# VectorE's order written out by hand while a two-layer kernel scans, and row scatters that no longer wait for each other

## The chip, the cores and the metric

The kernel runs on one core of one Trainium2 chip. The metric is the time of one execution on the device in microseconds (us). Three runs of the kernel before gave a median of 2133.94 us (2133.84 to 2136.27). The engines are named as the profile names them: PE (TensorE matmuls), PEld (TensorE weight loads), DVE (VectorE), ACT (ScalarE), POOL (GpSimd) and SP (SyncE, which here only issues DMAs).

## The reference

Two transformer-like layers run over 4 batches of 1024 tokens with 128 features. Each layer is an attention-like part and a mixture of experts, each behind a layer norm that is shifted, scaled and gated per batch. Layer 0 is causal attention with 16 heads, then 8 experts of which each token takes 2, without a capacity. Layer 1 is a selective scan (a Mamba block), then 8 experts, top 2, each with room for 512 tokens per choice. The part that the change is about is the scan:

```python
deltaA   = exp(delta[..., None, None] * A)                  # (B, S, 128, 16)
deltaB_u = delta[..., None, None] * B_sel[:, :, None, :] * u[..., None]
h   = a_t * h + bu_t                                        # for each token t in order
y_t = einsum('bdn,bn->bd', h, c_t)
...
x = x + ga * _L1_attn_ref(h, ...)    # silu(conv(x W_in)) scanned, gated by silu(z), times W_out
x = x + gb * _L1_ffn_ref(h, ...)     # router, top 2, gather, gelu experts, weighted sum
```

## The kernel before, in words

The residual `x` stays in SBUF as 32 tiles of 128 tokens. There are three stretches.

**Attention** (to about 1428 us of the profiled execution). Eight stages, one per batch and half of the heads. Layer 0's experts of a batch run beside the attention of the next one: `sort_tokens` (L331) ranks the tokens of a batch by expert and scatters their rows, 16 indirect DMAs issued by POOL (L385), into a DRAM tensor `f_in[b]` that was filled with zeros at the start (L491); `Blocks` (L393) multiplies 23 blocks of 128 rows; `return_steps` (L271) gathers the results back and DVE adds them to `x` (L278). The sort of batch 3, its blocks and the returns of batches 2 and 3 are left to the scan stretch. POOL also scales the probabilities (L586) that PE transposes (L595). All 16 scatters write one tensor, so each waits until the one before has landed.

**Scans** (1474 to 1906 us). A batch has 32 chunks: 16 groups of 8 features by 16 states, each for two halves of 512 tokens. A chunk (`scan`, L897) is a PE matmul that spreads `du` over the states into a PSUM bank `pu`, a DVE multiply by `bb` in place (L906), an ACT exponential `da` (L908), the DVE scan `h` (L910), for the first half an ACT copy of its last column into `carry` (L912), and a POOL multiply `hc` by `cc` (L914). There are four banks for `pu` and three buffers each for `da` and `h`. Four `hc` are summed by PE into `py` (`collected`, L917). After 16 chunks `scan_output` (L924) gates `py` into `yh` (L927), multiplies by `W_out` (`pw`), gates again (L932), and POOL adds to `x` (L934).

Other work goes beside the chunks, as generators that a `Beside` (L1159) advances by so many steps per pair of chunks from pair `at` on: `scan_inputs` of the next batch (L839: norm, convolution, softplus, `du`), `dispatch` of the batch before (L936: norm, router, top 2, positions, 16 scatters), the sort of batch 3, `first_blocks` (L774) and the returns. After the last pair of a batch every generator is run to its end (`f.rest()`) before the next batch's first chunk is written down.

**Layer 1's experts** (from 1941 us). `dispatch_last` handles the last four tiles, then 16 expert runs and the last blocks follow.

The order of instructions on every engine is made by the framework's scheduler from what the program writes down and its own estimate of durations; each engine then runs its list strictly in that order. The hand only breaks in with `next_to` and `issue_after`.

Of the kernel before, what the change touches and what calls it, by code (L numbers as in the profile page):

```python
# [49 lines left out]
def adaln_two_layers(ctx: ExitStack, tc: tile.TileContext, I: dict, out: bass.AP):  # L50
# [90 lines left out]
    def norm_steps(t0, nt, dst, on_act=True):  # L141
# [13 lines left out]
        yield  # L155

# [114 lines left out]
    def return_steps(src, t0, nt, placei, w, pool, bufs, store=False):  # L271

        came = []

        def add():
            for t, k, y in came:
                xt = x[:, t0 + t, :]
                nc.vector.scalar_tensor_tensor(xt, y, w[:, k, t : t + 1], xt, ALU.mult, ALU.add)  # L278
            if store and came and came[0][0] % 2 == 1:
                at = t0 + came[0][0] - 1  # L280
                nc.sync.dma_start(outv[:, at : at + 2, :], x[:, at : at + 2, :])

        for t in range(nt):
            here = []
            for k in range(2):
                y = pool.tile([P, D], F32, tag="fy", bufs=bufs, name="fy")
                nc.gpsimd.indirect_dma_start(
                    out=y,
                    out_offset=None,
                    in_=src[:, :],  # L290
                    in_offset=bass.IndirectOffsetOnAxis(ap=placei[:, k, t : t + 1], axis=0),
                )
                here.append((t, k, y))
            add()
            came = here
            yield
        add()

    kept = {}
# [11 lines left out]
    def first_returns(b, pool, bufs):  # L311
        _, placei, w = kept[b]
        return return_steps(f_out[b], b * TB, TB, placei, w, pool, bufs)
# [17 lines left out]
    def sort_tokens(b, kept, pool, ps, tag, xtag="fxn"):  # L331
# [5 lines left out]
        yield from feature_steps(xn, hT, ps, modT[0][:, 4, b : b + 1], modT[0][:, 3, b : b + 1])  # L337
        pl = ps.tile([P, TB, NE], F32, tag="m", name="fpl")
# [8 lines left out]
        pin = ps.tile([P, TB + 1, NE], F32, tag="m", name="fpin")  # L347
# [34 lines left out]
        kept[b] = expert, placei, w  # L382
        for t in range(TB):
            for k in range(2):
                nc.gpsimd.indirect_dma_start(  # L385
                    out=f_in[b][:, :],
                    out_offset=bass.IndirectOffsetOnAxis(ap=placei[:, k, t : t + 1], axis=0),
                    in_=xn[:, t, :],
                    in_offset=None,
                )  # L390
                yield

    class Blocks:  # L393


        def __init__(self, b, pool, ps, banks, rest):
            self.b, self.expert, self.pool, self.ps, self.rest = b, kept[b][0], pool, ps, rest
            self.banks = itertools.cycle(banks)
# [4 lines left out]
        def load(self, n):  # L403
# [3 lines left out]
            nc.sync.dma_start(self.xe[:, :m], rows_in[:, 3 * n : 3 * n + m])  # L407

        def turn(self, n):

            m = min(3, NB - 3 * n)
            tp = self.ps[0].tile([P, 3, P], F32, tag=self.ps[1], name="ftp")
# [8 lines left out]
        def first(self, j):  # L421

            if j >= NB:
                return
            w, r = self.ws[len(self.held)], j % 3
            bank, tag = next(self.banks)
# [5 lines left out]
            nc.scalar.activation(sg, pf[:, 0:2], AF.Tanh, scale=0.5)  # L432
            nc.vector.scalar_tensor_tensor(sg, sg, 1.0, pf[:, 0:2], ALU.add, ALU.mult)
# [4 lines left out]
            self.held.append((pf, am, ar))  # L438

        def second(self, j):  # L440

            if j >= NB:
                return
            w, r = self.ws.pop(0), j % 3
            pf, am, ar = self.held.pop(0)
            if r == 0:
                self.ye = self.pool.tile([P, 3, D], F32, tag="fye", bufs=1, name="fye")
            mm(nc, pf[:, 3], ar, w[:, 4 * P : 5 * P], stop=False)
            mm(nc, pf[:, 3], am, w[:, 3 * P : 4 * P], start=False)
            nc.vector.tensor_mul(self.ye[:, r], pf[:, 3], gate_b0[:, self.b, :])  # L450
# [12 lines left out]
    with ExitStack() as es:  # L463
# [23 lines left out]
        for slots in f_in + xd + [g_in]:  # L487
            flat = slots.rearrange("(p r) d -> p (r d)", p=P)
            for at in range(0, flat.shape[1], 512):
                n = min(512, flat.shape[1] - at)  # L490
                nc.sync.dma_start(flat[:, at : at + n], mask[:, :n])  # L491
# [169 lines left out]
        for at, (b, c) in enumerate(stages):  # L661
# [47 lines left out]
            if c == 0 and b > 0:  # L709
                blocks = Blocks(b - 1, ab, (ps_m, "m"), [(ps_m, "m")], rest)  # L710
# [26 lines left out]
    with ExitStack() as es:  # L737
# [36 lines left out]
        def first_blocks(b):  # L774

            blocks = Blocks(b, fb, (ps_g, "g"), [(ps_g, "g"), (ps_m, "d")], rest)
            for j in range(NB):
                if j % 3 == 0:
                    blocks.turn(j // 3)
                blocks.first(j)  # L780
                if j > 0:
                    blocks.second(j - 1)
                yield
            blocks.second(NB - 1)
# [54 lines left out]
        def scan_inputs(b):  # L839
# [23 lines left out]
            for t in range(TB):  # L863
                mm(nc, pd[:, t : t + 1], xc[:, t * P : (t + 1) * P], m_dt)
            r = mb.tile([P, TB], F32, tag="sp_r", name="sp_r")
# [31 lines left out]
        def scan(pair, g, carry, dt, du, bb, cc):  # L897

            tok = slice(g * 512, (g + 1) * 512)
            hcs, pus = [], []  # L900
            for c in pair:
                pu = ps_u.tile([P, 512], F32, tag=f"pu{next(turn) % 4}", name="pu")
                mm(nc, pu, spread[:, c].rearrange("p a n -> p (a n)"), du[:, tok])
                pus.append(pu)
            for c, pu in zip(pair, pus):
# [7 lines left out]
                hcs.append(wide("hc", 10, 512))  # L913
                nc.gpsimd.tensor_mul(hcs[-1], h, cc[:, tok])  # L914
            return hcs
# [8 lines left out]
        def scan_output(b, g, py, sz):  # L924
# [3 lines left out]
            pw = ps_m.tile([P, 4, D], F32, tag="d", name="pw")  # L928
            for q in range(4):
                mm(nc, pw[:, q], y[:, q * P : (q + 1) * P], m_out)  # L930
            u = mb.tile([P, 4, D], F32, tag="wide_gated", bufs=1, name="wide_gated")
            nc.vector.tensor_mul(u, pw, gate_a1[:, b : b + 1, :].to_broadcast([P, 4, D]))  # L932
            xt = x[:, b * TB + 4 * g : b * TB + 4 * g + 4, :]
            nc.gpsimd.tensor_add(xt, xt, u)  # L934

        def dispatch(b, t0, nt):  # L936
# [30 lines left out]
            mm(nc, pall.rearrange("p t k e -> p (t k e)"), ones, mine.rearrange("p t k e -> p (t k e)"))  # L967
            yield
# [42 lines left out]
        def dispatch_last():  # L1011
# [63 lines left out]
            for t in range(nt):  # L1075
                for k in range(2):
                    nc.gpsimd.indirect_dma_start(
                        out=g_in[:, :],
                        out_offset=bass.IndirectOffsetOnAxis(ap=placei[:, k, t : t + 1], axis=0),
                        in_=hx[:, t, :],  # L1080
                        in_offset=None,
                    )
# [7 lines left out]
        sent = []  # L1090

        def last_experts():
# [11 lines left out]
            def rows(q):  # L1104
                n = min(4, nb - q)
                ins[q] = eb.tile([P, 4, D], F32, tag="gxe", name="gxe")
                nc.sync.dma_start(ins[q][:, :n], rows_in[:, q : q + n])
# [51 lines left out]
        class Beside:  # L1159


            def __init__(self, steps, at, n):
                self.steps, self.at, self.n, self.value, self.ended = steps, at, n, None, False
# [15 lines left out]
        inputs = Beside(scan_inputs(0), 0, 1)  # L1179


        sending = None
        output = None
        for b in range(B):
            sz, xc, *scanned = inputs.rest()
            carry = mb.tile([P, NCH], F32, tag="carry", name="carry")
            beside, among = [], []
            if b == 0:
                beside.append(Beside(first_returns(B - 2, db, 6), 4, 1))
                beside.append(Beside(sort_tokens(B - 1, kept, db, ps_m, "hT2", "hx"), 2, 4))  # L1190
                beside.append(Beside(shift_and_scale(), NCH - 3, 1))
            if b == 1:
                among.append(Beside(first_blocks(B - 1), 1, 1))
            if b == 2:
                beside.append(Beside(first_returns(B - 1, db, 6), 0, 2))
            if sending is not None:
                beside.append(sending)
            if b + 1 < B:
                inputs = Beside(scan_inputs(b + 1), 5 if b == 2 else 2, 3 if b == 2 else 2)
                beside.append(inputs)  # L1200
            hcs, late = [], None
            for m in range(NCH):

                g, n = divmod(m, NCH // 2)
                hcs += scan([4 * (2 * n % 4 + r) + n // 2 for r in range(2)], g, carry, *scanned)
                for f in among:
                    if m >= f.at:
                        f.take(1)
                if n == 1:

                    if late is not None:
                        late()
                        late = None
                        if b + 1 == B:
                            beside.append(Beside(dispatch(b, 0, TB - NL), m + 1, 8))
                    elif output is not None:
                        output()
                        output = None
                if n == 2:
                    py = ps_y.tile([P, 512], F32, tag="py", name="py")  # L1220
                    mm(nc, py, skip, xc[:, g * 512 : (g + 1) * 512], stop=False)
                if n % 2 == 1 and n > 1:
                    collected(n // 2 - 1, hcs[:4], py)
                    hcs = hcs[4:]
                if n == NCH // 2 - 1:

                    def late(b=b, g=g, hcs=hcs, py=py, sz=sz):
                        collected(3, hcs, py)
                        scan_output(b, g, py, sz)

                    hcs = []
                for f in beside:
                    if m >= f.at:
                        f.take(f.n)
                for f in among:
                    if m >= f.at:
                        f.take(1)
            output = late
            for f in beside + among:
                f.rest()  # L1240
            if b + 1 < B:
                sending = Beside(dispatch(b, 0, TB), 2, 3)
            if b == 1:
                fw_scope.close()
                gw = ctx.enter_context(tc.tile_pool(name="gw", bufs=1, side="right"))
# [186 lines left out]
```

## Time and profile before

| | us |
|---|---|
| median of 3 runs | 2133.94 |
| profiled execution, own time | 2139.09 |
| its span, first to last instruction | 2137.4 |
| PE, DVE, POOL, ACT busy in the span | 1792.8, 1323.7, 994.6, 947.3 |
| scan stretch, first chunk to last `h` | 1474 to 1905.6 = 431.6 |
| last `h` to the first expert matmul `ph` | 1905.6 to 1941.1 = 35.5 |
| DVE multiply `pu` (L906), scan `h` (L910) | 0.684, 1.207 or 1.269 each |
| POOL `hc` (L914), one indirect DMA issue (L385) | 1.275, 0.99 each |

Busy times are unions of an engine's instructions; the rest of a stretch is idle time, and the profile names what ended each idle time. PEclk is the granted TensorE clock as a share of full speed.

### The profile page before, as it was taken

How to read it: one execution, taken by the hardware profiler on the slowest of the kernel's cores; microseconds unless marked ns; L12 is line 12 of the kernel's file. 1: busy time of each engine (PE TensorE's matmuls, PEld its weight loads, DVE VectorE, ACT ScalarE, POOL GpSimd, SP SyncE). 2: the span in 40 equal slices, each digit the busy share in tenths (PEclk: the TensorE clock that was granted, in tenths of full speed). 3: DMA queues.
4: the chain of work that ended last, by engine and by line, in shares of the span. 5: the costliest groups of instructions: out<-in, count | busy, mean ns of one | idle time of the engine just before them, and what ended most of it. 6: DMA issues, size and time to landing. Idle time of an engine off the chain costs nothing. (4 is left out here: it accounts for less than half of the span.)

```text
span 2137.4 us, 29054 instructions
## 1 busy us (share of the span) xinstructions
PE 1792.8 (84%) x8957; PEld 971.7 (45%) x8957; DVE 1323.7 (62%) x4000; ACT 947.3 (44%) x2073; POOL 994.6 (47%) x1277
## 2 busy tenths in 40 slices
PE   5399999998999989899989899967769757857984
PEld 3144344444455445455535446533335423325774
DVE  5356556665667666566766566655858888882243
ACT  1145454554445374355455454544456345423321
POOL 1334534436523643633363652344654675772254
PEclk9699999999999999999989999987979877867997
DMA  6400101001222200222210122210003230002345
GB/s 221 137 1 15 36 1 28 23 1 54 72 75 68 70 4 27 73 59 68 78 36 1 51 75 65 61 44 10 26 30 98 71 113 13 8 21 88 99 144 149
DMA packets 103756, 123.59 MB, mean 58 GB/s; under 512 B 15024, under 2 KB 68656, under 8 KB 103600
## 3 DMA queue, kind: packets, MB, share of 16 engines
q1 hardware_dynamic: 84256, 99.01, 15.7%
q0 software_dynamic: 8192, 16.74, 2.4%
q10 hardware_dynamic: 11152, 5.97, 0.9%
q8 instruction: 71, 1.16, 0.2%
q14 instruction: 85, 0.70, 0.1%
HBM read 67.85 MB, written 32.90 MB: 47 GB/s over the span
## 5 line engine op out<-in xcount | busy, mean ns | idle before, releaser
L586 POOL TENSOR_SCALAR pr<-pr,den 128x32 f32<-128x32 f32 (+31 forms) x512 | 353.2, 705 | 301.9 <-DVE den L583 295.9
L580 ACT ACTIVATE pr<-pr,nb 128x32 f32<-128x32 f32 (+31 forms) x512 | 371.6, 727 | 194.5 <-DVE nb L567 191.5
L595 PE MATMUL pt<-ident,pr 128*128 128x128 f32 x2304 | 341.9, 283 | 46.4 <-POOL pr L586 37.0
L46 PE MATMUL sc<-k,q 64*128 64x512 f32 (+14 forms) x1536 | 332.4, 525 | 41.4 <-DVE nb L567 24.4
L595 PEld LDWEIGHTS pt<-ident,pr 128*128 128x128 f32 x2304 | 253.8, 142 | 242.5 <-POOL pr L586 76.4
L46 PE MATMUL po<-pT,v 128*64 128x512 f32 x1152 | 345.9, 623 | 2.3 <-DVE pT L599 2.0
L597 ACT COPY pT<-pt 128x512 f32<-128x512 f32 x288 | 167.5, 582 | 356.8 <-PE pt L595 295.5
L567 DVE CUSTOM_DVE_ANT_0 pr<-sc,mask 128x512 f32<-128x512 f32 (+15 forms) x512 | 273.0, 559 | 76.2 <-PE sc L46 67.1
L599 DVE COPY pT<-pt 128x512 f32<-128x512 f32 x288 | 198.4, 689 | 166.1 <-PE pt L595 152.9
L46 PEld LDWEIGHTS sc<-k,q 64*128 64x128 f32 x1536 | 123.8, 193 | 197.6 <-DVE nb L567 93.3
L914 POOL TENSOR_TENSOR hc<-h,cc 128x512 f32<-128x512 f32 x128 | 161.6, 1275 | 108.7 <-DVE h L910 43.1
L46 PE MATMUL pu<-du,spread 128*128 128x512 f32 x256 | 146.4, 677 | 45.4 <-DVE h L910 41.0
L684 POOL MEMSET pr<- 128x288 f32 x128 | 42.4, 339 | 265.4 <-PE pt L595 261.3
L567 DVE CUSTOM_DVE_ANT_0 pr<-sc,mask,nb 128x416 f32<-128x416 f32 (+15 forms) x256 | 120.0, 496 | 7.0 <-PE sc L46 5.8
L908 ACT ACTIVATE da<-dt,negA 128x512 f32<-128x512 f32 x128 | 91.6, 719 | 66.1 <-DVE h L910 65.9
L46 PEld LDWEIGHTS po<-pT,v 128*64 128x64 f32 x1152 | 69.6, 136 | 84.4 <-issue 43.0
L503 DVE TENSOR_TENSOR rot_w<-proj,sin_sb 128x512 f32<-128x512 f32 x80 | 55.1, 688 | 76.7 <-PE proj L46 43.2
L906 DVE TENSOR_TENSOR pu<-pu,bb 128x512 f32<-128x512 f32 x128 | 85.2, 684 | 25.0 <-PE pu L46 14.9
L1300 POOL DMA_INDIRECT y<-slots_out,slot x56 | 56.5, 1009 | 93.8 <-PE ph L46 50.2
L46 PEld LDWEIGHTS pu<-du,spread 128*128 128x128 f32 x256 | 45.8, 207 | 115.4 <-DVE h L910 69.5
L545 POOL TENSOR_TENSOR q<-rot_u,rot_v 128x512 f32<-128x512 f32 x64 | 81.2, 1270 | 33.4 <-DMA rot_v<-rot_w 25.0
L580 ACT ACTIVATION_READ_ACCUMULATOR pr<-pr,nb 128x1 f32 x512 | 96.3, 188 | 0.0
(273 smaller groups left out, 2716.8 us busy)
## 6 DMA issues: line engine op xcount, KB each, us to landing
fw<-in_f_w SPq DMA_DIRECT2D x92, 320.0 KB
rot_v<-rot_w SPq DMA_DIRECT2D x320, 64.0 KB
gw<-in_g_w SPq DMA_DIRECT2D x15, 512.0 KB
fxe<-blocks_in SPq DMA_DIRECT2D x28, 192.0 KB
blocks_out<-fye SPq DMA_DIRECT2D x28, 192.0 KB
blocks_in<-mask SPq DMA_DIRECT2D x20, 256.0 KB
slots_in<-mask SPq DMA_DIRECT2D x16, 256.0 KB
g_w<-in_g_w SPq DMA_DIRECT2D x8, 512.0 KB
```

The costliest lines, as they stand in the source:

```text
L46: return nc.tensor.matmul(out, lhsT, rhs, start=start, stop=stop)
L545: nc.gpsimd.tensor_add(to, u.rearrange("p (n q) -> p n q", q=QG), v.rearrange("p (n q) -> p n q", q=QG))
L567: nc.vector.tensor_tensor_reduce(out=pr[hp][:, g, lo:hi], in0=sc[:, hp, : hi - lo], in1=mask[:, MW - hi + lo :] if hi == nk else mask[:, : ...
L580: nc.scalar.activation(p, p, AF.Exp, bias=nb[:, last, hp : hp + 1], scale=-1.0, accum_out=den[:, hp : hp + 1])
L586: nc.gpsimd.tensor_scalar(p, p, den[:, hp : hp + 1], 1.0, ALU.mult, ALU.mult)
L595: next_to(hp == 0 and g == 0, lambda: nc.tensor.transpose(to, p, ident))
L597: nc.scalar.copy(pT[:, hp, :], pt)
L599: nc.vector.tensor_copy(pT[:, hp, :], pt)
L906: nc.vector.tensor_mul(pu, pu, bb[:, tok])
L908: nc.scalar.activation(da, dt[:, tok], AF.Exp, scale=negA[:, c : c + 1])
L914: nc.gpsimd.tensor_mul(hcs[-1], h, cc[:, tok])
L1300: nc.gpsimd.indirect_dma_start(out=y, out_offset=None, in_=yd[k][:, :], in_offset=bass.IndirectOffsetOnAxis(ap=slot[:, k, t : t + 1], axis=0),
```

## The change

During the scans DVE runs in the order in which the program writes its instructions (`manual_schedule` for DVE); the other engines keep the scheduler. The program's text is rewritten for that:

- The loop advances the side work after every chunk instead of every pair, and a batch's side work is no longer run to its end at the batch's last pair: `inputs`, `returns`, `sorting`, `sends` and `blocks` are advanced one step per chunk (a dispatch two in the last batch) until they end, across the edges of batches. The sort of batch 3 and batch 2's returns start before the first chunk.
- Generators get extra `yield`s, and `Blocks` is cut into `hidden`, `gated`, `product` and `result`, so that what DVE reads was asked of PE or ACT one to three chunks earlier. `scan_output` is given in two steps, `collected` of the last four chunks and `yh` come in the next half's first pairs, and returned rows are added two steps after their gather (`lag=2`).
- The blocks use one bank of `pu` (`pu3`), so `pu` has three while the blocks run; `pw` moves to `py`'s bank, the sort to bank `g`.
- Scatters into `f_in[b]` and `g_in` no longer depend on each other; each depends on the zero fill, and the reads of the rows depend on all of them. Two scatters, not one, go into a step.

```diff
@@ norm_steps
         nc.scalar.activation(r0, r0, AF.Exp, scale=-0.5)
+        yield
         yield
@@ return_steps
-    def return_steps(src, t0, nt, placei, w, pool, bufs, store=False):
+    def return_steps(src, t0, nt, placei, w, pool, bufs, store=False, lag=1):
...
+            if len(came) == lag:
+                add()
...
+    def scatter(group, out, at, in_, fill):
+        ins = nc.gpsimd.indirect_dma_start(
+            out=out, out_offset=bass.IndirectOffsetOnAxis(ap=at, axis=0), in_=in_, in_offset=None
+        ).ins
+        if group:
+            tc.declare_no_dep(ins, group=group[0], reason="different rows")
+        else:
+            group.append(f"rows of {ins.name}")
+        tc.add_to_no_dep_group(group[0], ins)
+        after_all(ins, fill, "zeros")
+        group.append(ins)
+
+    def behind(read, group):
+        after_all(read.ins, group[1:], "scattered rows")
@@ sort_tokens
         for t in range(TB):
             for k in range(2):
-                nc.gpsimd.indirect_dma_start(
...
-                yield
+                scatter(arrived[b], f_in[b][:, :], placei[:, k, t : t + 1], xn[:, t, :], zeros[b])
+            yield
@@ first_blocks
+            blocks = Blocks(b, fb, [(ps_g, "g"), (ps_u, "pu3")], rest, 2)
+            blocks.turn(0)
+            blocks.hidden(0)
+            yield
             for j in range(NB):
-                if j % 3 == 0:
-                    blocks.turn(j // 3)
-                blocks.first(j)
                 if j > 0:
-                    blocks.second(j - 1)
+                    blocks.result(j - 1)
+                blocks.gated(j)
+                blocks.product(j)
+                if j + 1 < NB:
+                    if (j + 1) % 3 == 0:
+                        blocks.turn((j + 1) // 3)
+                    blocks.hidden(j + 1)
                 yield
@@ scan_inputs, before sp_r is read from pd: three more yields
@@ scan_output
-            pw = ps_m.tile([P, 4, D], F32, tag="d", name="pw")
+            pw = ps_y.tile([P, 4, D], F32, tag="py", name="pw")
             for q in range(4):
                 mm(nc, pw[:, q], y[:, q * P : (q + 1) * P], m_out)
+            yield
@@ the loop over batches
+        ordered.enter_context(tc.manual_schedule(engines={mybir.EngineType.DVE}))
+        while not inputs[0].ended:
+            for f in (inputs[0], returns[B - 2], sorting):
+                f.take(1)
...
+                free = 4 if blocks is None or blocks.ended else 3
+                for r, hc in enumerate(scan(pair, free, g, carry, *scanned)):
+                    hcs.append(hc)
+                    if n in (2, 3) and r == 0 and last is not None:
+                        if n == 2:
+                            giving = scan_output(*last)
+                        next(giving)
+                    if n == 4 and r == 1 and last is not None:
+                        if (b, g) == (B - 1, 1):
+                            sends.append(Beside(dispatch(b, 0, TB - NL), 2))
+                        elif g == 0:
+                            sends.append(Beside(dispatch(b - 1, 0, TB), 1 + b // (B - 1)))
+                        last = None
...
+                    for f in list(inputs.values()) + list(returns.values()) + [sorting] + sends[:1]:
+                        f.take(f.n)
...
-            for f in beside + among:
-                f.rest()
```

## The prediction

> **What bounds the kernel now.** I read the page's slices first: the scan stretch (1474 to 1905.6 us) is where neither PE nor DVE is full. Then I cut it by hand into the four batches and the gaps between them and asked for the busy time of each engine; the columns are the window, its length, then PE, PEld, DVE, ACT and POOL busy with instruction counts, the granted clock, DMA share and GB/s.
>
> ```profile
> 1474.00:1546.10 72.10, 61.30 (x203) 25.82 (x201) 66.82 (x109) 35.46 (x63) 43.98 (x36) 0.93 0.06 19
> 1546.10:1581.70 35.60, 18.11 (x47) 7.98 (x47) 9.47 (x58) 15.15 (x25) 17.02 (x17) 0.59 0.05 18
> 1581.70:1697.70 116.00, 98.89 (x459) 56.14 (x457) 94.86 (x195) 60.30 (x114) 62.15 (x54) 0.95 0.25 75
> 1697.70:1800.00 102.30, 71.68 (x258) 33.95 (x258) 87.75 (x176) 45.32 (x85) 70.71 (x60) 0.78 0.20 72
> 1800.00:1828.80 28.80, 19.59 (x70) 11.65 (x71) 10.94 (x52) 14.09 (x25) 22.78 (x20) 0.65 0.09 35
> 1828.80:1905.60 76.80, 53.84 (x164) 18.54 (x162) 74.03 (x117) 30.56 (x59) 56.52 (x47) 0.86 0.03 11
> 1905.60:1941.10 35.50, 13.18 (x53) 9.64 (x53) 21.30 (x84) 5.63 (x10) 20.06 (x19) 0.50 0.18 58
> ```
>
> Inside a batch DVE is nearly full (66.8 of 72.1, 74.0 of 76.8). Between batches 0 and 1 and between 2 and 3 it works 9.5 of 35.6 and 10.9 of 28.8 us: the next batch's inputs are a chain of small steps with nothing beside it. With blocks beside the chunks (1581.7 to 1697.7) it idles 21.1 of 116, PE 17.1. Over the 431.6 us DVE is busy 343.9, PE 323.4 at a mean clock of 0.84, POOL 273.2. So DVE is the engine to fill, and 431.6 - 343.9 = 87.7 us is all its idle time. The list of waits says what it idles for (waiter, releaser, us in total, times, longest):
>
> ```profile
> DVE pu L906 <- PE pu L46: 14.9, 7, 10.1
> DVE r_m L222 <- PE pl L46: 10.2, 4, 8.2
> DVE pu L906 <- ACT xn L172: 9.5, 1, 9.5
> DVE x L278 <- DMA fy<-blocks_out,f_placei: 7.9, 8, 2.3
> DVE yh L927 <- PE py L46: 7.6, 2, 7.3
> ```
>
> No wait dominates; together they are the answers that come late where no chunk was left to do meanwhile. In the attention stretch one wait belongs to the change. The waits of PE around the sorts of batches 0, 1 and 2 (485 to 540, 840 to 885, 1170 to 1235 us) begin with these lines, and POOL's own list has the last:
>
> ```profile
> PE pt L595 <- POOL pr L586: 7.8, 4, 6.5
> ```
>
> ```profile
> PE pt L595 <- POOL pr L586: 6.7, 2, 5.8
> ```
>
> ```profile
> PE pt L595 <- POOL pr L586: 8.0, 3, 4.8
> ```
>
> ```profile
> POOL blocks_in L385 <- DMA blocks_in<-fxn,f_placei: 47.7, 34, 3.2
> ```
>
> POOL stands still 47.7 us behind scatters in flight (9.9 of it in the scans), and the probabilities queued behind them come late to PE, 22.5 us in all.
>
> **The change part by part.**
>
> *DVE's work* hardly changes. From the first multiply to the last `h` the built program has 694 DVE instructions before and 703 after (some work of the gaps and of the tail changes sides): at the rows' durations 322.8 against 321.2 us, so 343.9 x 322.8/321.2 = 345.6. But small operations that ran in the quiet gaps now run beside `hc`. A row: `r_key` (L235, 128x64) takes 0.86 us in the chunks, while its 128x32 form takes 0.19 after the last chunk; softplus's `sp_s` (L830) has a median of 166 ns and a maximum of 1281. About 55 such operations leave the gaps. Between nothing and the 0.67 of L235 each (0 to 37 us) I take 0.13, 7 us, since most L830 stay near their median. The Trainium skill, "SBUF — State Buffer", "Who interferes with whom", says that a VectorE instruction with two SBUF inputs and a GpSimd one exclude each other for the whole instruction. That speaks against the change; with it each of the 55 would wait half of a 1.275 us `hc` while `hc` runs half of the time, 0.32 x 55 = 18 us by that estimate, 11 more than mine.
>
> *The gaps* vanish: inputs of batches 1, 2, 3 start at chunks 1, 33 and about 58 and need some 25 steps, so they end before chunks 33, 65 and 97. What is late next is a block: in the built order `gated` of block 0 stands after chunk 23 and block 22 ends at 47, 24 chunks with 70.2 us of DVE rows (75.1 scaled as above). I leave them the idle share of 1581.7 to 1697.7, 18%: 75.1/0.82 = 91.6. The rest, 345.6 - 75.1 + 7 = 277.5, gets 7%, the share of batch 0 (batch 3 has 4%): 277.5/0.93 = 298.4. Together 390.0, so the stretch gains **41.6**. Bounds: with no idle it is 352.6, a gain of 79; with all 87.7 kept, a loss of 9.
>
> PE is not the floor: its 323.4 include slow matmuls, `p<-dg,ones` at 1135 ns a pass against `pu` at its median 592, run where the clock is 0.59 to 0.65.
>
> *The added in-order waits.* Each answer that DVE reads now holds every multiply and scan behind it, and PE, ACT and POOL wait for those. I count 92: 46 by blocks, 14 by `scan_output`, 12 by three dispatches, 9 by inputs, 8 by returns, 3 by the sort. My 390.0 leaves 37.4 us of idle time, 0.41 each. The moved scatters (sort 16, 2 per chunk) and gathers (16) are still 0.99 and 0.95 of POOL each in POOL's order, and hold `hc`; SP's `fxe` read behind all 16 scatters holds only the weight loads behind it. Three `pu` banks instead of four under the blocks, and `pw` in `py`'s bank: nothing, since PE runs two chunks ahead of DVE still; without that cover a matmul pair (1.18 us) per chunk shows, 28 us at most, a gain excluded because a bank fewer frees nothing.
>
> *The tail.* Dispatch of batch 3's first half is written before `yh` and begins at chunk 126; before, its `pl` was read at 1896, 9 us before the last `h`. Its 36 small DVE operations, near 0.2 each, the exponential and `pin` (2.1) now stand ahead of `yh`, `pw` and the second half's norm. Before, `x` was added at 1921.8, 16 us after the last `h`; I reckon 21. **+5** (0 to +10). The prologue waits for the sort's 8 transposes, fxn (3.2) and fhT (1.5) on ACT, partly under softplus: **+2** (-1 to +5).
>
> *Scatters.* Issue stays 0.99 each; only the landing wait goes. Of PE's 22.5 us I take less than half, **-10** (0 to -22.5), since two scatters per step also make longer bursts ahead of a probability. For `g_in` 13.0 us of POOL waits go, from 1941 on, where PE is full of expert matmuls to 2060 and hides them: nothing, 13 at most.
>
> Sum: -41.6 + 5 + 2 - 10 = -44.6, from the profiled 2139.1 to 2094.5. The median lies 5.2 lower, so **2089**.
>
> **The rivals.**
>
> *Nearly full DVE* (0.10): all but 10 us of idle time goes, since batch 3 shows 96% busy: -69 + 7 - 16 = -78, 2056; to 2045 at the bounds. Against it: blocks keep PE near full.
>
> *POOL's bursts take it back* (0.13): in a burst 16 indirect issues and 8 `hc` need 16 x 0.99 + 8 x 1.275 = 26.0 us per 8 chunks, DVE's bare chunks 8 x 1.92 = 15.4; with three `h` buffers DVE waits. Four bursts (sort, returns, two dispatches) and half a fifth: 48 us on 345.6 + 7 + 15 = 415, a gain of 16, with +7 and -5: 2120. For it: 62.15 and 70.71 POOL in batches 1 and 2. Against it: small DVE work falls into the same chunks.
>
> *Slower* (0.13): one mechanism, the in-order read. In the scans before, DVE waited 62 times for about 85 us, 1.4 each. If the 92 reads cost that, 129 us stand on 352.6, 482 instead of 390: 2181. It decides from (431.6 - 352.6 + 3)/92 = 0.9 us per read. The scheduler also orders PE by estimated durations, so a wrong estimate puts one late answer in front of several chunks. Against it: the distance of one to three chunks is 2 to 6 us, and a matmul group and a table load with its activation last 2 each.
>
> *It does not do what it says*: the gaps go but the scheduler's order on PE and ACT brings the same idle time back, within 0.2% (0.04).
>
> **How the numbers follow.** Forecast 0.60, around 2089 (2070 to 2110). A measurement of this kernel can tell about 0.2%, 4 us, from no change. Faster 0.60 + 0.10 + 0.13 = 0.83, same 0.04, slower 0.13. The range reaches from 2045 (full DVE) to 2130 (POOL's bursts), and leaves out slower and same, 0.17.
>
> **What would show it.** Right: no stretch of 10 us without an `h` between the first and last chunk, DVE 88 to 92% busy, the clock above 0.88, `blocks_in <- DMA blocks_in` near zero, PE's wait for `pr` around sorts halved, last `h` to first `ph` near 40. POOL's bursts would show as `h <- POOL hc` of 30 us or more; the slower case as `yh`, `r_m`, `fsg`, `ln_r` waits above 0.9 each. A different order in the attention stretch, above 10 us either way, would break the sum.

## The result: slower, and the profile after

The changed kernel takes 2198.12 us (median of 4 runs, 2194.02 to 2202.78), the kernel before 2135.11 beside it: a ratio of 1.0292 (95% interval 1.0264 to 1.0321). The forecast was 2089, 46 us below the kernel before. The profiled execution after took 2202.78 us, with a span of 2201.0 against 2137.4.

The windows of the scan stretch again, cut at the first scan of each batch, and then the tail up to the first expert matmul; the columns are those of the windows of before:

```profile
1484.90:1611.40 126.50, 99.43 (x353) 50.63 (x353) 92.61 (x181) 57.01 (x102) 61.67 (x57) 0.80 0.17 54
1611.40:1750.40 139.00, 97.84 (x383) 49.64 (x386) 120.51 (x227) 58.71 (x109) 68.12 (x55) 0.86 0.22 73
1750.40:1855.90 105.50, 81.05 (x246) 34.13 (x238) 84.55 (x162) 53.81 (x95) 68.52 (x54) 0.79 0.03 11
1855.90:1957.10 101.20, 62.95 (x186) 23.47 (x186) 85.12 (x146) 34.48 (x68) 72.83 (x62) 0.75 0.04 17
1957.10:2001.30 44.20, 15.23 (x61) 11.39 (x61) 14.89 (x70) 7.92 (x13) 23.81 (x22) 0.50 0.16 51
```

The two quiet gaps are gone from the list, and yet the stretch is 472.2 us long instead of 431.2 (first multiply to the end of the last `h`). DVE is busy 382.8 us in it, 39 more than before, with 715 instead of 700 recorded instructions, and the clock is 0.81, not above 0.88. The waits of DVE in the stretch (waiter, releaser, us, times, longest) begin with an answer that cost 5.3 us before. First after, then the same read before:

```profile
DVE sp_r L921 <- PE pd L46: 27.4, 2, 19.3
DVE pu L961 <- PE pu L46: 11.2, 1, 11.2
DVE h L965 <- POOL hc L969: 8.4, 5, 3.2
DVE fsg L470 <- ACT fsg L465: 7.3, 6, 3.2
DVE x L280 <- DMA fy<-blocks_out,f_placei: 4.4, 2, 2.9
```

```profile
DVE sp_r L866 <- PE pd L46: 5.3, 2, 2.7
```

The 11.2 us of `pu` end with the first multiply and lie ahead of the stretch. The waits that came from the gaps did go: `pu` behind `xn` (9.5) and `yh` (7.6) are not in the list of after, and `r_m` fell from 10.2 to 2.3.

**DVE's own time.** A busy time does not tell what an instruction costs when it overlaps its neighbour. So I took from DVE's timeline, for each instruction, the time from its start to the next start, less the idle time the timeline names there. Over the stretch, in us (the tail runs from the last `h` to the end of the span):

| kernel | stretch | named idle | 128 multiplies | 128 scans | small operations | tail | ratio to before |
|---|---|---|---|---|---|---|---|
| before | 431.2 | 84.1 | 79.9 | 148.9 | 118.2 | 231.8 | 1 |
| after | 472.2 | 65.8 | 102.4 | 150.4 | 153.6 | 243.9 | 1.0292 |
| after, second profile | 472.7 | 65.0 | 102.3 | 150.5 | 155.0 | 245.2 | 1.0269 |
| e1_pairs | 472.4 | 84.5 | 77.1 | 150.2 | 160.6 | 229.0 | 1.0262 |
| e5_pin | 468.3 | 56.3 | 102.3 | 150.4 | 159.2 | 241.1 | 1.0238 |
| e7_pin_pairs_tail | 462.2 | 69.7 | 77.1 | 150.3 | 165.2 | 238.3 | 1.0199 |
| e11_dep | 480.7 | 72.8 | 102.6 | 150.3 | 155.1 | 240.0 | 1.0287 |
| e10_auto_dep | 401.5 | 47.7 | 80.8 | 150.6 | 122.4 | 239.7 | 1.0019 |
| e9_auto_dep_held | 421.2 | 59.9 | 80.3 | 149.5 | 131.5 | 244.1 | 1.0008 |

The runs of the first group (e1 to e4) have tails of 229 to 231 us, whether their edit touches the tail or not: from the first expert matmul to the end they need 185 to 186 us, where the other profiles need 195 to 201. So the tails of the first group are not set beside those of the others.

Idle time fell by 18.3 us; own time rose by 59.4: 22.5 of it in the multiplies, 35.4 in the small operations. Of the 406.4 us of own time after, 382.8 are busy; the rest are gaps of under 0.15 us, which the profile does not name as idle. The durations of the stretch's DVE instructions add up to 392.2 us before and 406.5 after, so most of the growth is not longer instructions: 45.4 us of them overlapped a neighbour before, 23.7 after. Before, DVE's timeline looks like this where chunks stand alone (start, us, engine, line; "x2" is two in a row):

```profile
1485.16 2.32 DVE L910 TENSOR_TENSOR_SCAN h<-da,pu 128x512 f32<-128x512 f32 x2
1487.40 1.27 DVE L906 TENSOR_TENSOR pu<-pu,bb 128x512 f32<-128x512 f32 x2
1488.58 2.32 DVE L910 TENSOR_TENSOR_SCAN h<-da,pu 128x512 f32<-128x512 f32 x2
```

and after:

```profile
1527.09 0.68 DVE L961 TENSOR_TENSOR pu<-pu,bb 128x512 f32<-128x512 f32 x1
1527.90 1.22 DVE L965 TENSOR_TENSOR_SCAN h<-da,pu 128x512 f32<-128x512 f32 x1
1529.03 0.67 DVE L961 TENSOR_TENSOR pu<-pu,bb 128x512 f32<-128x512 f32 x1
1529.84 1.22 DVE L965 TENSOR_TENSOR_SCAN h<-da,pu 128x512 f32<-128x512 f32 x1
```

Two multiplies in a row take 1.18 us to the next start, 0.59 each, though each lasts 0.69: an instruction starts before the end of one it does not read. After, each scan stands directly behind the multiply whose result it reads, and starts 0.81 us after it, 0.13 behind its end. Two chunks take 3.42 us before and 3.88 after. In the built order of after, 128 of 128 multiplies are followed at once by a scan; before it is 38, and there the median from start to start is 0.60 us, about what it is behind an instruction that is not read.

### The profile page after: what moved, and what is told of

It is laid out like the page before. It is cut to its first block, busy times and chain, and to the rows that moved or that the text cites. A ratio compares the mean times of both kernels' runs of the same rounds, so it can differ in the third digit from the quotient of the medians.

```text
span 2201.0 us, 29092 instructions
## 1 busy us (share of the span) xinstructions
PE 1824.3 (83%) x8957; PEld 983.6 (45%) x8957; DVE 1355.9 (62%) x4000; ACT 949.6 (43%) x2073; POOL 997.0 (45%) x1277
## 5 line engine op out<-in xcount | busy, mean ns | idle before, releaser
L46 PE MATMUL pu<-du,spread 128*128 128x512 f32 x256 | 167.8, 760 | 71.2 <-DVE h L965 57.9
L1355 POOL DMA_INDIRECT y<-slots_out,slot x56 | 56.6, 1011 | 102.9 <-PE ph L46 59.4
L961 DVE TENSOR_TENSOR pu<-pu,bb 128x512 f32<-128x512 f32 x128 | 87.9, 687 | 12.0 <-PE pu L46 11.2
```

The source lines that it names most:

```text
L46: return nc.tensor.matmul(out, lhsT, rhs, start=start, stop=stop)
L961: nc.vector.tensor_mul(pu, pu, bb[:, tok])
```

## The experiments

Ratios are to runs of the kernel before on the same chip in the same group. The first group ran on a chip where before took 2125.75 us, so its times in us are not set beside those of the others.

**e1_pairs: both multiplies ahead of both scans.**

```diff
-            for c, pu in zip(pair, pus):
+            for pu in pus:
                 nc.vector.tensor_mul(pu, pu, bb[:, tok])
+            for c, pu in zip(pair, pus):
                 da = wide("da", 3, 512)
```

> The changed kernel, with both multiplies of a pair of chunks ahead of both scans in DVE's program order; nothing else. Theory A (DVE's order itself costs: in the changed kernel each of 128 scans stands directly behind the multiply whose result it reads, and a multiply then takes 0.80 us from its start to the next start, against 0.63 before and 0.58 where two multiplies follow one another): 128 x (0.80 - 0.58) = 28 us less in the scan stretch, 2198 to 2170 - 2178 (ratio 1.016 to 1.020), and the multiply's share per chunk near 0.6 us. Theory B (other engines set the pace, and DVE's shorter work only turns into waits for PE, ACT or POOL): within 6 us of 2198, with POOL hc and PE pu waits of DVE longer by what the multiplies save.

Measured 1.0262 (1.0213 to 1.0311). The multiplies' own time fell as theory A said, by 25.3 us to 0.60 each. That the 0.81 came from the reading, and not from a scan following a multiply, shows here: a scan behind the multiply that it does not read starts after 0.60 us.

```profile
1488.23 1.29 DVE L961 TENSOR_TENSOR pu<-pu,bb 128x512 f32<-128x512 f32 x2
1489.42 1.21 DVE L966 TENSOR_TENSOR_SCAN h<-da,pu 128x512 f32<-128x512 f32 x1
```

The stretch did not follow (472.4), as theory B said: idle time rose by 18.7 and the small operations by 7.0. DVE's waits in the stretch of e1_pairs, behind 25.3 us of `sp_r`:

```profile
DVE pu L961 <- PE pu L46: 15.0, 5, 11.2
DVE h L966 <- POOL hc L970: 11.1, 7, 2.6
DVE fsg L470 <- ACT fsg L465: 10.4, 6, 3.2
DVE x L280 <- DMA fy<-blocks_out,f_placei: 6.4, 4, 2.9
DVE r_z L227 <- ACT r_s L225: 5.3, 2, 5.0
```

The same answers are waited for longer (`h` 11.1 us instead of 8.4, `fsg` 10.4 instead of 7.3): a DVE that reaches their readers sooner waits for them. So the 22.5 us are measured as a cost of the order, but undoing them alone buys almost nothing.

**e2_late_block: the first block asked for eight chunks later.**

```diff
-                    if blocks is None and sorting.ended:
+                    landed += blocks is None and sorting.ended
+                    if blocks is None and landed > 8:
                         blocks = Beside(first_blocks(B - 1))
```

> The changed kernel, with the first block of the last batch asked for eight chunks later, when the scattered rows have long landed; nothing else. Theory A (PE put the block's transposes, which wait for a load behind 16 scatters, ahead of the 8 pd matmuls of batch 1's inputs, and DVE reads pd in order with every scan behind it, 19.3 us once): 12 to 20 us less, 2178 to 2186, with the sp_r wait for pd below 10 us in all. Theory B (the blocks are a chain of their own that sets the length of the stretch, so a later start moves its end): no gain, or up to 8 us more.

Measured 1.0254 (1.0208 to 1.0301), inconclusive: the wait of `sp_r` for `pd` was still 23.6 us, since the scheduler moved the block's transposes on PE ahead of `pd` as before, wherever the program wrote them. Its profiled execution, at 2166.76 the fastest of its four, has a stretch of 463.0 us against 473.0 in e3_tail of the same group, but the medians of the two are 5 us apart with overlapping intervals. e5_pin repeats the test with PE's order held.

**e3_tail: the last `scan_output` ahead of the rest of the dispatch.**

```diff
-        for f in sends:
-            f.rest()
         collected(3, *last_hcs)
         drained(scan_output(*last))
+        for f in sends:
+            f.rest()
```

> The changed kernel, with the last scan_output written ahead of what is left of the dispatch of batch 3's first half; nothing else. Theory A (yh stands behind 36 DVE operations of that dispatch, which wait for pl, and pl's matmuls stand behind the last py, 12.3 us in all): the x add comes 16 to 20 us after the last h instead of 28, and the time falls by 6 to 12 us, to 2186 - 2192. Theory B (the last hc behind POOL's scatters sets the tail): within 4 us of 2198.

Measured 1.0279 (1.0231 to 1.0328): nothing. `yh` came 10.5 instead of 23.2 us after the last `h` and the addition to `x` 16.1 instead of 27.4, as theory A said, but the first expert matmul 42.8 instead of 44.2 (e1 and e2 too have 44.3 and 44.2). The gain it forecast did not come: the dispatch's operations, put behind, hold the first experts as much as `yh` held the last tiles.

**e4_auto: DVE left to the scheduler, all else as changed.**

```diff
-        ordered.enter_context(tc.manual_schedule(engines={mybir.EngineType.DVE}))
```

> The changed kernel with DVE left to the scheduler; loops, distances, banks and scatters as changed. Theory A (the order of DVE is what costs; the scheduler puts independent operations between a multiply and its scan and between dependent small operations): DVE's occupancy falls by 25 to 40 us, and the time to 2150 - 2175. Rival (the new loops, distances and scatters cost it, whoever orders DVE): 2190 to 2205. If the forecast of the gaps was right and only the order was wrong, below 2134.

Measured 1.0094 (1.0061 to 1.0128): most of the loss goes with this line. The multiplies' own time is back at 80.2 us. But the sort runs ahead of the first chunk (first multiply at 1507.4, 375 small operations in the stretch), so the stretch of 402.6 us cannot be set beside 431.2 as it is.

**after_again, e5_pin, e6_scatters, e7_pin_pairs_tail (one group).**

> The changed kernel itself, unaltered, as the anchor for the others of this group: 1.026 to 1.032 times the kernel before; its tail and its first multiply show how much of what the single edits seemed to move belongs to the chip they ran on.

Measured 1.0269 (1.0234 to 1.0303). Its stretch is that of the first profile within 0.5 us; its first multiply is at 1476.1, not 1484.9. So 9 us ahead of the scans differ between two executions of one program, and no term is read from there.

```diff
             for r in range(m):
-                nc.tensor.transpose(tp[:, r], self.xe[:, r], ident)
+                ins = nc.tensor.transpose(tp[:, r], self.xe[:, r], ident)
+                if self.outs == 2 and n == 0 and r == 0:
+                    tc.keep_in_program_order(ins)
```

> The changed kernel, with the first transpose of the last batch's first block held behind the PE work written before it, so that the 8 pd matmuls of batch 1's inputs go first. The late start of the earlier experiment left PE's order as it was and so decided nothing. Theory A (one transpose, waiting for a load behind 16 scatters, held PE, and with it pd and every scan behind pd's reader on DVE): the 19 us wait of sp_r for pd falls below 6, and the time by 10 to 19 us against the unaltered changed kernel. Theory B (the blocks' chain sets the stretch, and the same 9 us are waited for elsewhere): within 5 us of it.

Measured 1.0238 (1.0207 to 1.027), 7 us below after_again by the medians, with overlapping intervals. What e5_pin undoes is this piece of PE's timeline in after (the last column is the idle time in front, and what ended it):

```profile
1545.72 1.02 PE L46 MATMUL pu<-du,spread 128*128 128x512 f32 x2
1555.60 0.90 PE L443 MATMUL ftp<-ident,fxe 128*128 128x128 f32 x3 [8.86 <-DMA fxe<-blocks_in]
1556.29 3.41 PE L46 MATMUL pd<-m_dt_sb,xc 128*128 128x1 f32 x16
```

PE stood 8.9 us in front of a transpose whose rows had not landed, `pd` behind it, and on DVE `sp_r` and every scan behind `pd`: no `h` from 1540 to 1560. So 8.9 of the 19.3 us are this wait for rows; the rest is other work that PE's list has ahead of `pd`, and `pd` itself. Held behind `pd`, the longest such wait falls from 19.4 to 8.7 us, not below 6, and the stretch by 4.4.

e6_scatters puts the change's `scatter`, `behind` and `zeros` into the kernel before, and nothing else.

> The kernel before, with only the scatters of sorts and of g_in made independent of one another (waits of POOL for scatters in flight gone); order, loops, distances and banks as before. As forecast for this part: 5 to 22 us less than before (2113 to 2129 where before is 2135), with blocks_in <- DMA blocks_in gone and PE's wait for pr around sorts below half of 22.5 us. Rival (bursts of scatters and other engines' orders give it back): within 4 us of before, or slower.

Measured 1.0055 (1.0033 to 1.0077): slower. The mechanism worked (PE's wait for `pr` around the sorts is 10.0 us instead of 22.5), and what it gave was taken back. At the third sort the softmax is 3.8 us earlier than before (ACT's 429th exponential of the probabilities, 1181.8 against 1185.6), and then ACT's next normalised tokens, for the same single buffer, stand in front of the probabilities' copies and wait for the last scatters:

```profile
1204.89 0.88 ACT L172 ACTIVATE fxn<-x,ln_away,ln_r 128x128 f32<-128x128 f32 x2 [7.91 <-DMA blocks_in<-fxn,f_placei]
```

Behind that wait the 437th exponential is 10.0 us later than before (1223.4 against 1213.4). The first multiply is at 1475.0 (1474.4 before), and the stretch then takes 438.9 us, 7.7 more; the small operations' own time is 8.2 longer there (126.4), and why is open.

e7_pin_pairs_tail joins the edits of e1, e3 and e5.

> The changed kernel with three edits together: both multiplies of a pair ahead of both scans, the first block's transpose held behind pd, and the last scan_output ahead of what is left of the dispatch. Pairs alone took 25 us off DVE's occupancy and nothing off the stretch, since its waits grew by 19 us. If that was because the late pd and the chain of side work set the pace (theory A), the pin sets the pairs free: 25 to 40 us less than the unaltered changed kernel. If waits for answers refill whatever DVE gives up (theory B), no more than the pin alone by over 6 us.

Measured 1.0199 (1.0169 to 1.0229), 10 us below the pin alone: between the two theories. The pairs give DVE 25.2 us again; 13.4 come back as idle time and 6.0 in the small operations.

**e9, e10, e11, e12 (one group).** e11_dep undoes the independent scatters in the changed kernel. e10_auto_dep is e11_dep without the `manual_schedule` line. e9_auto_dep_held is e10_auto_dep with the sort and returns started behind the first scans:

```diff
-            for f in (inputs[0], returns[B - 2], sorting):
-                f.take(1)
+            inputs[0].take(1)
...
+                        with tc.issue_after(first_h[-1]) if f is sorting else nullcontext():
+                            f.take(f.n)
```

> The changed kernel with the scatters dependent on one another again, DVE in program order as changed. If the scatters cost here what they cost the kernel before (12 us): 1.020 to 1.024 against 1.027 to 1.029 for the unaltered changed kernel. Rival, as forecast: they are worth 10 us, and without them it is 1.031 to 1.034.

> The changed kernel with DVE left to the scheduler and the scatters dependent on one another again. The independent scatters alone cost the kernel before 0.55 per cent, DVE left to the scheduler gave 1.0094. If the two add up: 1.002 to 1.006 of before. If independent scatters only hurt in the old loops: 1.008 to 1.011.

> The changed kernel with DVE left to the scheduler, the scatters dependent on one another again, and the sort of the last batch and the first returns held behind batch 0's first scans, as in the kernel before. What stays of the change is its loops: chunk-wise side work with two and three chunks between asking and reading. Left to the scheduler the first multiply came at 1507 instead of 1474 us, since the sort ran ahead of it, and the stretch took 403 instead of 431. Theory: the first multiply returns to 1474 - 1480, the stretch takes 415 to 425, and the time is 0.994 to 1.002 of before, a version that may beat both. Rival: the sort's early start is what shortened the stretch, and the stretch goes back to 430 or more: 1.002 to 1.010.

Measured: e11_dep 1.0287 (1.026 to 1.0314), e10_auto_dep 1.0019 (1.0004 to 1.0034), e9_auto_dep_held 1.0008 (0.9992 to 1.0024). e11_dep and e10_auto_dep, which differ in one line, are 2.7% apart, 56 us by the medians. In e10_auto_dep the first multiply comes only at 1496.6, as in e4_auto, so its stretch cannot be set beside the others either, and e9_auto_dep_held serves for that. The windows of the stretch, first e11_dep, then e9_auto_dep_held:

```profile
1474.00:1954.80 480.80, 342.95 (x1162) 157.63 (x1161) 384.16 (x715) 205.10 (x374) 271.10 (x227) 0.82 0.13 41
```

```profile
1467.80:1889.00 421.20, 313.94 (x1183) 144.04 (x1181) 357.57 (x728) 207.53 (x384) 262.09 (x218) 0.87 0.14 46
```

With the same loops, distances and scatters, but the sort and the returns started later, the stretch is 59.5 us shorter, with more DVE instructions in it: 22.3 in the multiplies, 23.6 in the small operations, 12.9 in idle time. Against the kernel before it is 10.0 shorter, and the tail 12.3 longer.

In program order the scatters make no difference to the time (1.0287 against 1.0269 and 1.0292): e11's rival and its theory both fell. But the wait moved. With dependent scatters the last one of batch 3's sort is issued at 1563.0 instead of 1550.8, and DVE stands in front of the first block's `gated`:

```profile
1571.25 0.42 DVE L463 SCALAR_TENSOR_TENSOR fsg<-fsg,pf 128x256 f32<-128x256 f32 x1 [21.72 <-ACT fsg L458]
```

In after as in e11_dep that read stands behind 23 chunks, whenever the rows land; in the kernel before it stands behind 40, in e9_auto_dep_held behind 51, and the longest wait for `fsg` is 1.6 and 1.3 us. The `manual_schedule` line also leaves PE's and ACT's lists to be made anew around DVE's, so the 56 us belong to the whole order it brings, not to DVE's own time alone.

e12_no_wide sends the tokens to the slots without row scale and shift, which leaves that part of the computation out:

```diff
-            nc.gpsimd.tensor_mul(hs, hx, row["scale"][:, b : b + 1, :].to_broadcast([P, nt, D]))
-            nc.gpsimd.tensor_add(hs, hs, row["shift"][:, b : b + 1, :].to_broadcast([P, nt, D]))
+            hs = hx
```

> The changed kernel without POOL's multiply by the row scale and addition of the row shift in the dispatches (2.35 us each); the slots receive the normalised tokens as they are, so this part of the computation is left out. Theory (small operations of DVE stand still while POOL runs such operations back to back: 5.53 us of an operation of 0.17 ended with POOL's third operation in a row): the small operations' durations fall by 8 to 14 us, single ones of 3 us and more are gone, and the time falls by 6 to 15 us. Rival (those stalls lie where DVE would have waited anyway): durations fall, the time stays within 5 us of the unaltered changed kernel.

Measured 1.0241 (1.0219 to 1.0262). The case it aims at, in POOL's timeline of after and then in DVE's:

```profile
1699.05 2.36 POOL L1003 TENSOR_TENSOR hs<-hs,row_shift 128x1024 f32<-128x1024 f32 x1
1701.35 1.27 POOL L969 TENSOR_TENSOR hc<-h,cc 128x512 f32<-128x512 f32 x1
1702.58 2.35 POOL L1065 TENSOR_TENSOR x<-x,gate_bias 128x1024 f32<-128x1024 f32 x1
```

```profile
1699.43 5.53 DVE L874 TENSOR_SCALAR sp_w<-sp_e 128x8 f32<-128x8 f32 x1
1704.99 0.20 DVE L875 RECIPROCAL sp_w<-sp_w 128x8 f32<-128x8 f32 x1
```

An operation on 128x8 lasts from POOL's first to POOL's third operation. In e12_no_wide it takes 0.94 us, and the small operations' durations in the stretch fall by 4.0 us against the first profile of after and 5.5 against the second, less than the 8 to 14 forecast; one of 3.81 remains, now beside the `gate_bias` addition, and the stretch is 471.3, as long as in after: the rival holds for the stretch. What the ratio gains, 6 us on after_again with overlapping intervals, lies in the tail (237.7 against 245.2).

**e13_early, e14_best: the last dispatch begun a pair earlier and taken four steps per chunk, as changed and in e9_auto_dep_held.**

```diff
-                    if n == 4 and r == 1 and last is not None:
+                    if n == (3 if (b, g) == (B - 1, 1) else 4) and r == 1 and last is not None:
-                            sends.append(Beside(dispatch(b, 0, TB - NL), 2))
+                            sends.append(Beside(dispatch(b, 0, TB - NL), 4))
-                            sends.append(Beside(dispatch(b - 1, 0, TB), 1 + b // (B - 1)))
+                            sends.append(Beside(dispatch(b - 1, 0, TB), 1 + 3 * (b // (B - 1))))
```

> The changed kernel with the dispatch of batch 3's first half begun one pair of chunks earlier and taken four steps per chunk, as fast as in the kernel before, and the dispatch ahead of it also at four steps; nothing else. The stretch from the last scan to the end took 244 us as changed and 232 before, also where DVE was left to the scheduler (244). Theory (it is the late begin of this dispatch, at chunk 126, that makes the tail long): the tail falls to 232 - 236 and the time by 6 to 12 us against the unaltered changed kernel's 2195 - 2198. Rival (the tail is paid by what stands ahead of yh in DVE's order, or by POOL's scatters): the tail stays above 240.

> The kernel of the new loops with DVE left to the scheduler, dependent scatters and a held sort (1.0008 of before), with the same earlier and faster last dispatches. Theory: its tail falls from 244 to 232 - 236 with the stretch near 421: 0.994 to 0.998 of before, faster than both. Rival (the dispatch's work only moves from the tail into the scans, which are full): 0.999 to 1.002.

Measured 1.0271 (1.0214 to 1.0327) and 0.9996 (0.9975 to 1.0018). In e13_early the tail fell to 216.3 us, further than forecast, and the stretch rose to 494.0: the work only moved, in e14_best too (237.5 and 425.3). No version here is faster than the kernel before beyond its interval.

## Why the prediction was wrong, by its own steps

- **Where the miss lies.** The span grew by 63.6 us instead of falling by 44.6. The stretch has 41.0 of it (-41.6 forecast), the tail 12.1 (+5), and what lies ahead of the first multiply 10.5 in this profile (-8 for the scatters and the prologue).
- **What bounds the kernel.** The 87.7 us of idle time were read rightly, but 10.1 of the first listed wait (`pu` behind `pu`, 14.9) ended with the first multiply and so lie ahead of the stretch. That DVE is the engine to fill was half the truth: e4 to e11 show that its order decides what filling it costs.
- **"DVE's work hardly changes"** is the step that failed. It scaled the busy time of before by the instructions' durations, 345.6 + 7 = 352.6 us, and so took the overlap that the scheduler's order had as kept. DVE's own time in the stretch became 406.4, 53.8 more (busy 382.8). The order moved scans and small operations directly behind those they read. That there was an overlap to lose stood in the trace of before: 3.42 us for two chunks, whose instructions last 3.8. It is the larger part of the stretch's miss of 82.6; the other, 28.4, is idle time.
- **The price of small operations beside POOL.** I took 7 us for about 55 operations, from one row of `r_key` at 0.86; its eight rows of that form in the scans of before run from 0.22 to 1.19, 0.72 in the mean. The 319 small operations that both stretches have in the same number and form last 108.8 us before and 122.3 after, 13.5 more, not all of it shown to be POOL's doing; their own time grew from 92.3 to 119.9, so half of that, 14.1, is not longer instructions but overlap lost and short gaps. The Trainium skill, "SBUF — State Buffer", "Who interferes with whom", gave 18 by the estimate in the prediction; 13.5 lies between. Its rule has the blocked side wait for the whole instruction of the other; the 5.53 us here cover three of POOL's.
- **Idle time.** 390.0 - 352.6 = 37.4 us forecast, 65.8 measured; 27.4 of these are two reads of `pd`. The other 38.4 have the forecast's size; that they are the waits it meant is not shown. The fault that can be named is the sentence that `fxe`, read behind all 16 scatters, "holds only the weight loads behind it" on SP: on PE its transpose held `pd`, for 8.9 of the 19.3 us, and in e11_dep the same rows held DVE for 21.7. That DVE's order would be hand-written and PE's not was known, and what PE would put ahead of a read answer was not looked up.
- **The tail**, +5 (0 to +10): +12.1, of which 8.7 lie ahead of the first `ph`, inside the bounds; the 3.4 behind it are not explained (the two profiles of after differ there by 1.4). As forecast the dispatch stands ahead of `yh`. What was missed is that it itself waits: `pl`'s matmuls stand on PE behind the last `py`, which waits for POOL. DVE, then PE, after the last scan of after:

```profile
1955.81 1.28 DVE L965 TENSOR_TENSOR_SCAN h<-da,carry,pu 128x512 f32<-128x512 f32 x1
1969.41 0.19 DVE L223 TENSOR_REDUCE r_m<-pl 128x4 f32<-128x32 f32 x1 [12.32 <-issue]
```

```profile
1965.64 1.93 PE L46 MATMUL py<-hc,gather 128*32 128x512 f32 x8 [8.27 <-POOL hc L969]
1967.50 1.88 PE L46 MATMUL pl<-g_rw_sb,hT 128*128 128x8 f32 x8
```

  The first `ph` comes 44.2 us after the last `h` (35.5 before; "near 40" was named). That the dispatch stands ahead of `yh` is not what costs: with DVE left to the scheduler (e4, e9, e10) `yh` starts 3.5 us after the last `h`, and the first `ph` still comes after 44.7 to 45.0. e13, where `ph` comes after 18.0 and the stretch is 21.8 longer, shows that it is the dispatch's work itself, which the old loop did among the last chunks.
- **Scatters**, -10: the mechanism as said, the sign wrong. `blocks_in <- DMA blocks_in` is gone, and PE's wait for `pr` around the sorts fell from 22.5 to 7.1 us, more than halved. The three windows after:

```profile
PE pt L640 <- POOL pr L631: 3.1, 4, 1.7
```

```profile
PE pt L640 <- POOL pr L631: 2.0, 2, 1.1
```

```profile
PE pt L640 <- ACT pT L642: 11.0, 1, 11.0
PE pt L640 <- POOL pr L631: 2.0, 3, 1.2
```

  The 11.0 us are new: ACT's `fxn` waits 13.0 us for the scatters' reads of the same buffer, and the copies `pT` wait behind it. Alone the edit costs 0.55%; in the changed kernel nothing shows.
- **The prologue**, +2: the first multiply, which holds the scatters' -10 as well, moved from 1474.4 to 1476.1 in the second profile and 1484.9 in the first, so +1.7 or +10.5 where the two terms together say -8, with 9 us that the program does not explain. The larger figure is over the 10 us that the prediction named as breaking its sum.
- **The rivals.** The slower one had the right side and 2181, near 2198 by luck: it put 129 us of waiting on 352.6, and measured are 65.8 on 406.4. The 62 waits it starts from are 56 in the list of before, for 84 us. It needed 0.9 us per in-order read, and 65.8 / 92 is 0.7, less idle time than before in all; only its single late answer in front of several chunks is seen, in `pd`. POOL's bursts stayed small (`h <- POOL hc` 8.4 us). That DVE's own time might grow by more than the small operations' 0 to 37 us was in no rival. Of the signs of being right, `blocks_in` and `pr` came; DVE is busy 81% of the stretch, not 88 to 92, and there are 20 us without an `h`.
- **Not settled:** how much of the 56 us is DVE's own time and how much is late answers. Pairs gave 25 us of own time for 0 to 10 us of the kernel's time; the scheduler's order gave 46 us of own time and 13 of idle time for 60 (e11 against e9). Small operations interleaved one by one under a hand-written order were not tried. The granted clock in the stretch is 0.84 before, 0.81 after and 0.87 in e9_auto_dep_held; whether it has a part in the time was not tested either.

## What to carry to other kernels

Before an engine's order is taken from a scheduler, count in the built order how often an instruction stands directly behind one that it reads, and price it by the distance of starts in the trace, not by its duration. A hand-written order on one engine needs the other engines' orders looked up for every answer it reads: one early instruction there, or a read written ahead of the landing of its rows, stops everything behind the reader. And here shortening the busy engine alone paid little: 25 us less of its own time bought 0 to 10 us.

## What the runs showed of the hardware

- A DVE instruction of 0.69 us lets the next one start after 0.59 if that does not read it, and after 0.81 if it does (`pu` and `h`, timelines above; 0.60 in e1_pairs, where the scan reads another multiply). The Trainium skill, "Perfetto Trace Analysis", "Optimizing Scalar/DVE Operations", says that the write-acknowledgement half of an instruction's latency overlaps with the next instruction; the 0.59 agrees that there is an overlap, and the 0.81 bounds it to a next instruction that does not need the result.
- A small DVE operation can be held through a whole run of POOL operations: 5.53 us over three different ones, and in e9_auto_dep_held 4.34 us, to the end of three `hc` in a row (3.74 together).
- Two profiled executions of one program reached the first multiply 8.8 us apart and then took 472.2 and 472.7 us for the same stretch.
